# Layer 0 of a convolution-attention hybrid: the first spectral product worked on modes, without a forward transform of q, with a skip matrix from TensorE and image sums in four tiles

## The chip, the cores and the metric

The kernel runs on one core of one Trainium2 chip. The metric is the device time of one execution in microseconds (us). One core has five engines with instruction queues of their own: PE (TensorE, matrix products; PEld are its weight loads), DVE (VectorE), ACT (ScalarE), POOL (GpSimd) and SP (SyncE, which here only issues DMAs). They wait for each other by semaphores.

## What is computed

The input x is [4, 32, 128, 128] in float32: four images of a batch, each with T = 32 channels of 128 x 128 points. Two layers follow each other. Layer 0 is a neural-operator block with attention; layer 1 is an attention and a mixture of experts over tokens. Only layer 0 is concerned here. Cut to what matters, it computes per image of the batch:

```python
def _spectral_conv(x, w):                 # keep 64 x 33 modes, multiply, go back
    X = rfft2(x); Xk = low modes of X
    return irfft2(Xk * w)                 # (for one channel: a product per mode)

x0 = _gn(x)                               # group norm
xn = _inorm(x0)                           # each channel's image to mean 0, variance 1
k, q, v = (_spectral_conv(xn, W) + skip * xn for W, skip in (K, Q, V))   # 32 heads
p_attn = softmax(q . k)                   # between the 32 channels, for each head
p = _spectral_conv(p_attn . v, Pcw) + skip # back from the heads to one
a  = _inorm(p + x0)
an = _inorm(a)
m = gelu(_inorm(_spectral_conv(an, m0cw)) + m0sw * an)
m =      _inorm(_spectral_conv(m,  m1cw)) + m1sw * m
x = x + _inorm(m) + a
```

"The first spectral product" is the one with m0cw. Its input, called q in the kernel (the code reuses the letter for p + x0), is itself a sum: what the attention makes in modes, plus a matrix over the 32 channels times x. So its modes can be had in two ways: by a forward transform of the finished q, or from the attention's own modes plus the same small matrix times the modes of x, which the kernel has from the start of the image.

## The kernel before

All matrix products are float32. A transform is two products with tables in SBUF: over columns, then over rows. The loop `for b in range(B)` (L912) goes through the four images; the front of image b + 1 (its norms and modes) is put into the second half of image b. A tile scheduler sets the order of each engine's queue from the program order and its own costs, and `behind(later, earlier)` adds an order by hand. The parts of one image, in order of time, are these.

- *The mix, u stage* (L955 to L1015). For each of five blocks of 13 (last 12) rows of modes and each of four groups of 8 channels, SP loads the modes of x, broadcast over partitions, as a pair of `xb` (L969, one for the real and one for the imaginary part; the pool holds four pairs), ACT copies them to PSUM as `xw` (L980), POOL (L989) or DVE (L993) multiplies them with the weights `gb` into `u`, and PE sums with the softmax `pr` into `po` (L926). In between PE transposes the image (`pxt`) and multiplies it with the channel matrix `bd` (`sk`), which gives the skip part of q. The pairs are loaded from `xd` in DRAM, written by SP (L559) when the image's modes are ready.
- *py, pv, four* (L1022 to L1048). py goes from channel-major to the layout for the inverse transform (L1027), ACT and DVE copy it to `yf`; `inverse` (L313) makes `pv` (L319) and `four` (L324), and DVE adds the result to q and takes its statistics (L1042, L1044).
- *q's norm and forward transform.* `stats("q", st)` (L258) packs the statistics (`pk`), sums them on PE (`m`) and takes the mean mode apart (`x0`, `flat`, `dq`). `spectra(0, q)` (L1101) transforms q: rows on PE (L305), copies `z`, columns on PE (L1123, `px`), the multiplication by the masks on DVE (L1134, L1137) and the sum on POOL (L1140, `spec`). `weighed` (L1150) gets the variance of the product from the squares (L1085, L1091, L1099) with one more PE sum, `ms`. From it come `r0`, `hq`, `hb`, `hs`, the scales of the gelu.
- *The next image's sums*, `image_rows` (L389): ACT squares (L395), PE sums image and square over blocks (L401, 32 products of 512 columns into two tiles of 32 output rows), ACT copies `ev` (L410), and `image_moments` (L413) spreads them with 16 small products (L419).
- *The gelu stage* (L1195 to L1245). `row_products` (L334, L342) and `four_images` (L353, L358) bring the product back, `gelu(a, g)` adds the skip part on DVE (L1212), ACT applies the gelu (L1216) and DVE takes statistics (L1224). `early` rows of the second transform (L305 with g) go between. `add_attention` (L1076, L1079) adds scaled q to the image, 32 adds in all.
- *The second norm and product.* `stats("gl", st)` again has pk, m and x0; `spectra(1, gl)` transforms g. Beside it the front of the next image runs: `spectra_of_images` (L482) with the column scales `colg` (L448), the products L503, L523, L534, the writes of `xd` (L559) and an edge row (L564), then `attention_weights` (L653): scores, softmax `ph` (L755), `prd` and `pr` through DRAM (L771, L775).
- *The end of the image.* The inverse of the second product (`back`, L360) runs in two halves, a = 0 and a = 1; its results are added to the image (L1334 on POOL, L1399 on DVE) and stored as x1 in four stores of 512 KB (L1422). `skip_matrix` (L780) makes `bd` for the next image from ph: two products cm (L787), two DVE products and two reductions of 512 elements (L791, L792), and bd (L797). It is called after half a = 0.

For image 0 there is no image before it: its front runs alone at the start, and `spread_values` (L629) makes the weights gb for all images from 64 products gw (L638), with copies on DVE and ACT (L644, L646).

Of the kernel before, what the change touches and what calls it, by code (L numbers as in the profile page):

```python
# [36 lines left out]
def _constants():  # L37
# [55 lines left out]
    )  # L93
    return by_p.astype(np.float32), inv_cols.astype(np.float32)
# [5 lines left out]
NCONST = 128 + 128 + NX + 2 * NU + 4 + 32 + 4 + 96 + 64 + P + 32 + 3 * NY + 2 * P  # L100
# [30 lines left out]
def layer0(  # L131
    tc, x, kq_modes, kq_mirror, v_modes, v_mirror, pcw, mcols, mrows, heads, heads_by_row, heads_row, small_row, by_p, inv_cols, dram, x1, first
# [57 lines left out]
    cos_back, sin_back = columns(P), columns(P)  # L190
    par = const.tile([P, NSMALL], F32, name="par")
# [5 lines left out]
    nc.vector.memset(one_of_8[:, 7:8], 1.0)  # L197
    ones = const.tile([P, P], F32, name="ones")
# [59 lines left out]
    def stats(name, st):  # L258
# [11 lines left out]
        m = ps.tile([P, 2, T], F32, name="m", tag="wide")  # L270
# [5 lines left out]

        x0 = ps.tile([P, 2, T], F32, name="x0", tag="wide")
# [23 lines left out]
    def four_rows(images, z, k, copy):  # L301

        pz = ps.tile([P, 4, P], F32, name="pz", tag="a")
        for j in range(4):
            nc.tensor.matmul(pz[:, j], images[k + j], rows, start=True, stop=True)  # L305
        return copy(z[:, k : k + 4], pz)
# [27 lines left out]
    def row_products(spec, a, ahead=(), slots=range(4), wide=None):  # L334

        wide = wide or [ps.tile([P, 2, 512], F32, name="y1", tag="wide") for _ in range(2)]
        for slot in slots:
            c = slice(slot * P, slot * P + P)
            for k, trig in enumerate((cos_back, sin_back)):
                for g in range(4):  # L340
# [8 lines left out]
                    for earlier in ahead:  # L349
                        behind(mm, earlier)  # L350
        return wide
# [37 lines left out]
    def image_rows(xt):  # L389

        products = []
        rows8 = ps.tile([64, 4, C], F32, name="rows8", tag="a")
        for g in GROUPS:
            xx2 = grp.tile([P, GI, C], F32, name="xx2", tag="pr", bufs=6)
            square = nc.scalar.activation(xx2, xt[:, g : g + GI], AF.Square)  # L395
            if "q_r" in roots:
                behind(square, roots["q_r"])
            for h in range(2):
                m = g // 4 + h
                for k, src in enumerate((xt[:, 4 * m : 4 * m + 4], xx2[:, 4 * h : 4 * h + 4])):  # L400
                    mm = nc.tensor.matmul(  # L401
                        rows8[32 * k : 32 * k + 32],
                        one_of_8[:, 7 - m : 39 - m],
                        src,
                        start=m == 0,
                        stop=m == 7,
                    )
                    products.append(mm)
        ev = grp.tile([64, 4, C], F32, name="ev", tag="pr", bufs=6)
        nc.scalar.copy(ev, rows8)  # L410
        return ev, products

    def image_moments(ev):  # L413

        s12 = [ps.tile([P, T], F32, name=f"s{t}", tag="a") for t in "ab"]
        for j in range(4):
            for k in range(2):
                r = slice(32 * k, 32 * k + 8)
                nc.tensor.matmul(s12[k][:, j::4], ev[r, j], ident[r, r], start=True, stop=True)  # L419
# [62 lines left out]
    def spectra_of_images(b, xt, normed, then=None):  # L482
# [6 lines left out]
        xd = dram.tile([T, 2, KX + 1, KY], F32, name=f"xd_{b}")  # L489
        xe = modes.tile([P, KP, T + T // 2], F32, name=f"xe_{b}", tag="xe")  # L490
# [4 lines left out]
        folded = {}  # L495

# [14 lines left out]
        def unfold(a):  # L511
# [44 lines left out]
            nc.vector.tensor_copy(xx[:1, t, 0], bias)  # L556
            for part in range(2):
                for x0 in (32, 0):
                    nc.sync.dma_start(  # L559
                        out=xd[t, part, 32 - x0 : KX - x0].rearrange("t x y -> x t y"),  # L560
                        in_=xx[KX * part + x0 : KX * part + x0 + 32, t, :KY],
                    )

        def edge_row():  # L564
# [6 lines left out]
            nc.vector.tensor_tensor(x32, o32, ysc[:m], ALU.mult)  # L571
            w32 = small.tile([m, T], F32, name="w32", tag="w32")
            nc.vector.tensor_scalar(w32, x32, edge[:m], None, ALU.mult)
            t32 = ps.tile([T, m], F32, name="t32", tag="a")
            nc.tensor.matmul(t32, x32, ident[:m, :m], start=True, stop=True)
            s32 = small.tile([T, 2 * n], F32, name="s32", tag="s32")
            nc.scalar.copy(s32[:, :m], t32)
            nc.sync.dma_start(
                out=xd[:, :, KX], in_=s32.rearrange("t (r y) -> t r y", r=2)[:, :, :KY]
            )  # L580
            return x32, w32
# [22 lines left out]
        return xx, (xe, xm), xd, edges, ysc, by_group  # L604

    def value_weights():
        shape = [P, KX // 4, KA]
        t1, t2 = (prep.tile(shape, F32, name=f"v{n}", tag=f"t{n}") for n in (1, 2))
        for ri, op in enumerate((ALU.add, ALU.subtract)):
            c0 = v_raw[:, :, 0, ri]  # L610
# [301 lines left out]
    for b in range(B):  # L912
# [122 lines left out]
        if b == 0:  # L1035
            mode_tables(weighed_last)
# [1078 lines left out]
```

## Time and profile before

| | us |
|---|---|
| median of 3 runs | 2871.71 (2871.12 to 2872.87) |
| the profiled execution | 2870.23 |
| its span, first to last instruction | 2868.6 |
| layer 0 | 0 to 833 |
| start of py (L1027), images 0 to 3 | 131.55, 323.99, 515.20, 707.76 |
| first gelu (L1216), images 0 to 3 | 186.43, 377.66, 569.29, 764.54 |

The mean clock granted to TensorE is 0.985 of full speed. Where lines of the profile are shown below, a line of the time line reads: start in us from the span's start, busy us, engine, line of the kernel, operation, out <- in, shape of the output <- shape of the input, how many instructions the line sums up, and in brackets how long the engine stood idle ahead of it and what ended that wait. SPq is the issue of DMAs on SP, with the time SP spent issuing, not the transfer's. Durations of products of PE on small tiles overlap, so their mean is longer than the distance between them.

### The profile page before, as it was taken

The numbers are of one execution on the slowest core, as the hardware profiler recorded it, in microseconds if no ns is written. First come the engines' busy times: TensorE is split into PE (matmuls) and PEld (weight loads), VectorE is DVE, ScalarE is ACT, GpSimd is POOL, SyncE is SP. The second block draws the span as 40 slices with busy tenths as digits, with TensorE's granted clock in tenths as the row PEclk, the third lists the DMA queues.
The fourth block names the chain that finished last, engine by engine and source line by source line (L and its number), as shares of the span: only waits on it lengthen the run. The fifth ranks groups of instructions, "written<-read, shape, count | busy, mean of one in ns | idle before, by whom it ended". The sixth has DMA issues, their size and how long they took to land.

```text
span 2868.6 us, 52910 instructions
## 1 busy us (share of the span) xinstructions
PE 2720.7 (95%) x19638; PEld 1379.6 (48%) x19638; DVE 2175.5 (76%) x4830; ACT 2315.7 (81%) x3243; POOL 2035.3 (71%) x1804
## 2 busy tenths in 40 slices
PE   8898999988879999999999999999999999999996
PEld 5565664654644444445444444544444454444442
DVE  5888788778766677777787776778788677877777
ACT  3555466465459999999999999999999999999990
POOL 2706418137028998998998988898898888878872
PEclk9999999999989999999999999999999999999998
DMA  4403204114030101002101000110100010010000
GB/s 103 125 1 106 88 8 149 39 42 138 3 81 23 41 1 41 8 14 47 40 2 34 16 16 19 41 27 23 41 1 16 20 34 19 16 34 1 16 12 19
DMA packets 151153, 107.72 MB, mean 38 GB/s; under 512 B 36302, under 2 KB 140017, under 8 KB 150897
## 3 DMA queue, kind: packets, MB, share of 16 engines
q1 hardware_dynamic: 147633, 102.26, 13.5%
q8 instruction: 155, 2.54, 0.4%
q10 hardware_dynamic: 3264, 2.10, 0.3%
q14 instruction: 101, 0.83, 0.1%
HBM read 63.86 MB, written 19.50 MB: 29 GB/s over the span
## 4 chain that ended last, share of the span: by engine, by line
PE 60%; ACT 7%; DVE 5%; POOL 3%; issue 2%; DMA 0%; SPq 0%; DVEq 0%; POOLq 0%; ACTq 0%
PE d L1869 26%; PE po L1888 15%; PE px L1770 6%; PE n L1869 5%; ACT r L1938 3%; DVE r L1943 1%; ACT e L1954 1%; DVE xc L1779 1%; ACT r L1950 1%; PE pl L1739 1%; POOL e L1946 1%; PE pz L1571 1%; PE pa L1701 1%; PE pt L1533 1%; PE pz L1586 1%
## 5 line engine op out<-in xcount | busy, mean ns | idle before, releaser
L1943 DVE TENSOR_TENSOR r<-n,r 128x1024 f32<-128x1024 f32 (+1 forms) x1056 | 961.9, 953 | 457.3 <-PE n L1869 327.9
L1938 ACT ACTIVATE r<-d 128x1024 f32<-128x1024 f32 (+1 forms) x1056 | 793.6, 803 | 63.6 <-PE n L1869 51.4
L1946 POOL TENSOR_TENSOR e<-r 128x512 f32<-128x512 f32 x528 | 673.4, 1275 | 213.0 <-DVE r L1943 211.4
L1950 ACT ACTIVATE r<-r 128x1536 f32<-128x1536 f32 x528 | 783.6, 1484 | 16.8
L1947 POOL TENSOR_TENSOR e<-e,r 128x512 f32<-128x512 f32 x528 | 671.8, 1272 | 41.4
L1869 PE MATMUL d<-qe,ke 32*128 32x512 f32 (+3 forms) x2304 | 604.5, 601 | 16.9 <-ACT r L1938 12.8
L1869 PE MATMUL n<-qe,ke 32*128 32x512 f32 (+3 forms) x2304 | 604.6, 601 | 0.0
L1888 PE MATMUL po<-e,kx 128*128 128x512 f32 (+3 forms) x1152 | 594.4, 605 | 3.0 <-POOL e L1959 3.0
L1869 PE MATMUL n<-qf,kf 32*128 32x512 f32 (+3 forms) x2304 | 550.8, 553 | 0.0
L1869 PE MATMUL d<-qf,kf 32*128 32x512 f32 (+3 forms) x2304 | 549.1, 552 | 0.0
L1779 DVE SCALAR_TENSOR_TENSOR xc<-px,wgt,xc 128x128 f32<-128x128 f32 x1024 | 354.5, 349 | 34.9 <-PE px L1770 5.2
L1888 PEld LDWEIGHTS po<-e,kx 128*128 128x128 f32 x1152 | 175.4, 188 | 376.1 <-issue 297.6
L1954 ACT ACTIVATE e<-e 128x512 f32<-128x512 f32 x528 | 324.2, 614 | 14.7 <-POOL e L1947 14.7
L1869 PEld LDWEIGHTS d<-qe,ke 32*128 32x128 f32 x2304 | 176.5, 183 | 302.0 <-ACT r L1938 273.2
L1869 PEld LDWEIGHTS d<-qf,kf 32*128 32x128 f32 x2304 | 219.1, 185 | 164.4 <-issue 152.6
L1770 PE MATMUL px<-we,x2t 128*128 128x512 f32 (+3 forms) x644 | 271.0, 515 | 5.7 <-DVE xc L1779 2.0
L989 POOL TENSOR_TENSOR u<-xb,gb 128x858 f32<-128x858 f32 (+1 forms) x112 | 220.6, 2008 | 42.4 <-PE po L926 37.6
L1869 PEld LDWEIGHTS n<-qf,kf 32*128 32x128 f32 x2304 | 227.5, 185 | 24.8 <-issue 17.2
L1140 POOL TENSOR_TENSOR spec<-part,part 128x512 f32<-128x512 f32 x16 | 25.7, 1609 | 284.8 <-DVE gn_r_t L253 93.0
L993 DVE TENSOR_TENSOR u<-xw,gb 128x858 f32<-128x858 f32 (+1 forms) x208 | 215.6, 1105 | 6.7 <-ACT xw L980 3.1
L1770 PEld LDWEIGHTS px<-we,x2t 128*128 128x128 f32 x644 | 119.3, 193 | 140.4 <-issue 116.8
L1869 PEld LDWEIGHTS n<-qe,ke 32*128 32x128 f32 x2304 | 176.8, 183 | 10.9 <-DVE r L1943 1.5
(425 smaller groups left out, 3409.3 us busy)
## 6 DMA issues: line engine op xcount, KB each, us to landing
xb<-xd SPq DMA_DIRECT2D x128, 214.5 KB
xc<-x SPq DMA_DIRECT2D x29, 512.0 KB
x<-x SPq DMA_DIRECT2D x16, 512.0 KB
qf<-qe SPq DMA_DIRECT2D x64, 128.0 KB
out<-xc SPq DMA_DIRECT2D x15, 512.0 KB
x<-in_x SPq DMA_DIRECT2D x14, 512.0 KB
xb<-xd SPq DMA_DIRECT2D x32, 198.0 KB
kf<-ke SPq DMA_DIRECT2D x32, 128.0 KB
```

The source lines that it names most:

```text
L989: weighed = nc.gpsimd.tensor_tensor(u, xb, gk, ALU.mult)
L993: weighed_last = nc.vector.tensor_tensor(u, xw, gk, ALU.mult)
L1770: nc.tensor.matmul(px[:, at_e : at_e + m], x2t[:, k * P : (k + 1) * P], we[:, own[0] : own[0] + m], start=True, stop=True,)
L1779: nc.vector.scalar_tensor_tensor(xc[:, k], px[:, i], wgt[:, k, e : e + 1], xc[:, k], ALU.mult, ALU.add)
L1869: nc.tensor.matmul(o, k, q, start=turn == 0 or g > 0, stop=turn == 1 or g > 0)
L1888: nc.tensor.matmul(sums[c, h][:, q0 : q0 + c1 - c0], kx[:, jb], e[:, c0:c1], start=jb == 0, stop=is_last and q0 > 2 * P, skip_group_check= ...
L1938: nc.scalar.activation(r[:, g], d, AF.Ln, scale=1.0 / DSCALE)
L1943: nc.vector.tensor_tensor(r[:, g], part, r[:, g], ALU.mult)
L1946: nc.gpsimd.tensor_tensor(e, r[:, 1], r[:, 2], ALU.add)
L1947: nc.gpsimd.tensor_tensor(e, e, r[:, 0], ALU.add)
L1950: nc.scalar.activation(r, r, AF.Exp, scale=-1.0)
L1954: nc.scalar.activation(e, e, AF.Exp)
```

## The change

The parts of the diff belong together as follows.

- The front of an image keeps its unscaled modes too: ACT copies them to `plain`, and eight DMAs write them to a second buffer `xu` in DRAM, behind those of `xd`; `edge_row` makes a second edge row for it. In the mix, eight DMAs read them back as `xs`, in the layout of py, put between the loads of xb.
- py accumulates: `rows_of` puts the attention's part into PSUM and has ACT copy it to yf for the inverse, and `first_product` adds `by_part` times `xs` to the same PSUM tile. DVE multiplies it with two columns of the mode table, and POOL adds the two into `modes_of_q`: these are the modes of the first spectral product.
- The forward transform of q, its masks, `dq` and the mean mode of `stats("q")` go. The variance of the product is the sum of the squares of `modes_of_q` (one Square on ACT, one reduction on DVE, two corrections for the zero columns, one PE sum).
- The inverse is made from `modes_of_q` by four channels at a time: pv2 and fours (128 products), in place of `row_products` and `four_images`. The gelus run in the order of channels. The adds of `add_attention` stand at other places: eight ahead of gelu(0), eight after gelu(1), sixteen after the last gelu.
- `image_rows` uses four tiles of 32 output rows, `image_moments` eight products with `one_row`; the squares are made between the copies of yf.
- `skip_matrix` makes cm with 32 products of one column and spreads it by one product with `alike`; it also makes `by_part`, and is called after half a = 1.
- `stats` leaves out the mean mode for q; the tables for masks, mirrors and constants change with these.

Cut to its core:

```diff
-    def image_rows(xt):
+    def image_rows(xt, parts, earlier=None):
...
-                    mm = nc.tensor.matmul(
-                        rows8[32 * k : 32 * k + 32],
+                    r = 64 * k + 32 * (m % 2)
+                    mm = nc.tensor.matmul(
+                        rows8[r : r + 32],
                         one_of_8[:, 7 - m : 39 - m],
                         src,
-                        start=m == 0,
-                        stop=m == 7,
+                        start=m < 2,
+                        stop=m > 5,
...
-                r = slice(32 * k, 32 * k + 8)
-                nc.tensor.matmul(s12[k][:, j::4], ev[r, j], ident[r, r], start=True, stop=True)
+                r = slice(64 * k, 64 * k + 64)
+                nc.tensor.matmul(s12[k][:, j::4], ev[r, j], one_row[r], start=True, stop=True)
...
+            plain = grp.tile([P, half, KY], F32, name="plain", tag="fold")
+            nc.scalar.copy(plain.rearrange("p (k i) y -> p i k y", i=2), std[:, :, :, :KY])
+            unscaled.append((t, plain))
...
+        for t, plain in unscaled:
+            to_rows(xu, t, plain)
+        store_edge(*edge_rows[1])
...
-            cm = ps.tile([P, T, 16], F32, name="cm", tag="a")
-            mm = nc.tensor.matmul(cm, pv[r].to_broadcast([NH, P]), ph[r], start=True, stop=True)
...
+            for t in range(16):
+                j = 32 * (t % 4)
+                mm = nc.tensor.matmul(
+                    cm[j : j + 32, t // 4 : t // 4 + 1], ph[r, :, t], pv[r], start=True, stop=True
+                )
...
+        nc.tensor.matmul(cp[:, 0], alike, by_four.rearrange("p h k j -> p (h k j)"), start=True, stop=True)
+        nc.vector.scalar_tensor_tensor(cp[:, 1], cp[:, 0], own, same, ALU.mult, ALU.add)
...
+                if x0 and by_images:
+                    to, of = by_images.pop(0)
+                    nc.sync.dma_start(out=to, in_=of)
...
+            copied = nc.scalar.copy(yf[:, :, :, y0 : y0 + n].rearrange("p t r y -> p y r t"), pys[y0])
...
+        def first_product(y0):
...
+                    nc.tensor.matmul(
+                        py[r, k], xs[r, :, y0 + k], by_part[r], start=False, stop=k == n - 1, skip_group_check=True
+                    )
...
+            nc.vector.tensor_tensor(one_, py, table[:, :, :1].unsqueeze(3).to_broadcast(shape), ALU.mult)
+            nc.vector.tensor_tensor(
+                two, py[:, :, ::-1], table[:, :, 1:].unsqueeze(3).to_broadcast(shape), ALU.mult
+            )
+            nc.gpsimd.tensor_tensor(
+                modes_of_q[:, :, :, y0 : y0 + n].rearrange("p t r y -> p y r t"), one_, two, ALU.add
+            )
...
+        nc.scalar.activation(squares, modes_of_q.rearrange("p t r y -> p t (r y)"), AF.Square)
...
+        nc.vector.tensor_reduce(by_t, squares, AX.X, ALU.add)
...
+        energy_of = sums("ms", ones, by_t, "b")
...
-        spec, sq = spectra(0, q)
-        ahead = []
-        if b + 1 < B:
-            ev, ahead = image_rows(loaded)
-        v0 = weighed("v0", sq, squares, layers[0][2], "a")
-        if ahead:
-            behind(summing["ms"], ahead[-3])
...
+        for k in range(4):
+            inverse_of(k)
+        add_attention(0)
+        gelu(0)
+        if b + 1 < B:
+            ev, _ = image_rows(loaded, next_squares, roots["gelu"])
+            sv = image_moments(ev)
+        gelu(1)
+        add_attention(GI, roots["gelu"])
+        inverse_of(4)
+        inverse_of(5)
+        gelu(2)
+        gelu(3)
+        inverse_of(6)
+        inverted = inverse_of(7)
+        for k in range(4, 8):
+            gelu(k)
+            early_rows(k - 4)
...
-        for g in GROUPS:
-            add_attention(g)
+        for g in GROUPS[2:]:
+            add_attention(g, roots["gelu"])
...
-            if a == 0 and b + 1 < B:
-                bd = skip_matrix(weights[2], front[4], inverted)
+            if a and b + 1 < B:
+                bd, by_part = skip_matrix(weights[2], front[4], rows_last)
```

## Prediction, made before the changed kernel ran

> **What bounds the kernel now.** I read the busy totals first, then busy time by stretches of one image, then the time lines of single engines. TensorE is busy 95% of the span, but only layer 0 (0 to 833 us) is touched; layer 1 is an unchanged program that starts later or earlier as a block. So the question is how long one image of layer 0 takes. Image 1, from the start of its py products at 131.55 to the same products of image 2 at 323.99, takes 192.4 us. Cut at the points where the chain changes hands (columns: stretch, length, busy PE, PE load, DVE, ACT, POOL with counts, clock, DMA share, GB/s):
>
> ```profile
> PE 2720.7 (95%) x19638; PEld 1379.6 (48%) x19638; DVE 2175.5 (76%) x4830; ACT 2315.7 (81%) x3243; POOL 2035.3 (71%) x1804
> ```
>
> ```profile
> 131.55:158.70 27.15, 25.82 (x284) 24.58 (x285) 18.36 (x73) 7.10 (x10) 0.00 (x0) 1.00 0.01 2
> 158.70:186.40 27.70, 26.14 (x273) 15.57 (x271) 23.54 (x94) 13.11 (x25) 3.45 (x2) 1.00 0.00 1
> 186.40:203.60 17.20, 13.89 (x120) 8.67 (x122) 15.24 (x66) 15.43 (x40) 0.00 (x0) 1.00 0.01 1
> 203.60:234.00 30.40, 28.58 (x321) 23.49 (x312) 24.89 (x101) 14.73 (x48) 4.36 (x4) 0.97 0.07 11
> 234.00:265.50 31.50, 26.69 (x286) 13.16 (x284) 22.86 (x33) 20.95 (x49) 23.44 (x14) 0.98 0.46 109
> 265.50:324.00 58.50, 52.63 (x643) 25.74 (x642) 54.08 (x53) 36.17 (x82) 51.02 (x26) 1.00 0.56 172
> ```
>
> The reader is to see that the first two and the fourth stretch are carried by TensorE (over 94% busy), the third by DVE and ACT (the gelus), and the last by DVE and POOL together: a pause there isn't caught up. In the time line these lines are the joints:
>
> ```profile
> 131.55 8.03 PE L1027 MATMUL py<-cst,rs 128*64 128x64 f32 x132 [0.61 <-ACT rs L1013]
> ...
> 158.71 0.20 DVE L263 TENSOR_TENSOR pk<-st 128x32 f32<-128x32 f32 x1
> ...
> 179.96 0.38 PE L383 MATMUL ms<-v_s,ones 128*128 128x32 f32 x2
> ...
> 186.43 3.19 ACT L1216 ACTIVATE g<-g,hb,hs 128x128 f32<-128x128 f32 x8
> ...
> 204.99 0.40 PE L271 MATMUL m<-pk,ones 128*128 128x64 f32 x2
> ```
>
> q is normed at 158.71, but the first gelu waits until 186.43, because the variance of the spectral product (ms, 179.96) comes only after q's forward transform (L305, L1123) and next to the next image's sums (L401, 32 records). From the start of py to the first gelu the four images take 54.9, 53.7, 54.1 and 56.8 us.
>
> At the other end of the image, on SP's queue and on DVE:
>
> ```profile
> 238.29 7.79 SPq L969 DMA_DIRECT2D xb<-xd  x8
> 254.84 2.96 SPq L771 DMA_DIRECT2D prd<-ph  x4
> 258.54 1.64 SPq L775 DMA_DIRECT2D pr<-prd  x2
> 260.28 1.08 SPq L1422 DMA_DIRECT2D x<-x  x2
> 263.24 1.22 SPq L969 DMA_DIRECT2D xb<-xd  x2
> 267.07 2.20 SPq L1422 DMA_DIRECT2D x<-x  x2
> ```
>
> ```profile
> 257.28 0.69 DVE L791 TENSOR_TENSOR cd<-cm,sel 128x512 f32<-128x512 f32 x1 [0.43 <-PE cm L787]
> ...
> 260.94 1.97 DVE L797 TENSOR_TENSOR bd<-cst,cp 128x128 f32<-128x128 f32 x1
> ...
> 266.96 8.71 DVE L993 TENSOR_TENSOR u<-xw,gb 128x858 f32<-128x858 f32 x9
> ```
>
> Four pairs of xb are loaded ahead of the softmax, and the skip matrix (257.28 to 262.9) stands in front of the last four adds, so the unbroken run of u products starts at 266.96.
>
> **What the Trainium skill says.** "TensorE: Matmul & The Clock Gate", Architectural detail: DVE and ACT take their queues strictly in order. So an add that isn't urgent delays everything behind it; the trace agrees (the adds at 262.84 come straight after bd). The same page, Part 3, Measured speedup: three column tiles give 2.38 times. In the trace the two 32-column tiles of L401 already run in pairs, 0.43 us apart. "DMA: Bandwidth & Descriptors", Issuing engines are not separate DMA queues: all transfers share the 16 DMA engines and interleave. The trace agrees so far as two 512 KB stores and the xb loads around them share the stretch of DMA share 0.46 to 0.56.
>
> **The change part by part**, against the profiled run (2870.23 us, span 2868.6).
>
> 1. *py to q's norm: +5.* 66 more products of two records each go into the same PSUM as py. 132 records of py took 8.03 us; 64x64 records elsewhere go at 0.026 (32 of em in 0.83), so these cost 132 x 0.026 = 3.4 to 8.0; I take 5. They stand ahead of the pv products on PE, so q is late by this. The two DVE multiplications of each group (0.68 each) and the POOL add (1.27 to 2.18) run beside PE's next products. q's norm: T + 27.2 + 5 = T + 32, with T the start of py.
>
> 2. *From the norm to the first gelu: -14.* The transform of q goes: 32 row products (7.1 us of PE), px (4.3), the two row products' place ahead of the gelus, the masks, weights and reduction on DVE. The variance is now a Square of 2112 elements on ACT and a reduction on DVE (about 2.1 and 2.3 us, scaled from 1.05 for 1024 and 1.21 for 1024), and ends during q's own inverse. What is left is the chain of small operations: m, three inverse roots (each about 2.5 us, as 161.94 to 164.5), pk and m (1.6), some ten DVE steps of 0.2, what eight adds between them push aside (about 1.4), the table load 1.28: pk + 13.8 against pk + 27.7. So the first gelu comes at T + 45.8: 9.1, 7.9 and 8.3 us earlier for images 0 to 2. The next image's sums in four column tiles (32 records, about 4 instead of 8.4 us of PE) and half as many moment products stand beside this.
>
> 3. *The gelu stage: +0.8.* 17.16 us become about 18: eight adds (0.265) and the inverse of pv2 and fours (128 records, 14.2 us of PE against 11.1) come in; DVE and ACT had 1.8 us free each, PE 3.3. Last gelu: 8.3, 7.1 and 7.5 us earlier, 22.9 in sum.
>
> 4. *Adds ahead of the second norm: +3.3 for each of three images.* The order of DVE now has 14 adds of groups 2 and 3 behind the last statistics and before pk: 14 x 0.265 = 3.7 us. PE's m, at 204.99 now, waits, and behind it in PE's order the rest of the transform of g and the next image's front, in a stretch where PE is 94% busy. Bounds 1 (PE still has row products when g ends) and 4. Sum 9.9.
>
> 5. *End of the attention: +2.3 for each of three images.* Behind the eight xd writes eight more writes (xu, the unscaled modes) and an edge row are put; they run 8 us more (1.0 us each, as xd), before the softmax is done, at no cost. But the scheduler now has only one pair of xb ahead of the four x1 stores; the others stand behind them. The skip matrix, now 32 one-column products and small DVE steps, stands behind the last adds, so the stores can go at about 261 instead of 267. 2 MB at the 280 GB/s that the trace reaches take 7.5 us, a pair of xb (429 KB) 1.5, and 1.5 from issue to landing: the second pair is there at 270.5, copied at 271.5. DVE has done three u by then, of 52: 49 x 1.1 from 271.5 ends at 325.4 to 326.3, against 324.0. Bounds 0 and 7. Sum 6.9. For image 0 there are no stores.
>
> 6. *Reads of xs in the u stage: +0.3 an image, 1.2.* Eight reads of 135 KB go between the xb; DMA share there is 0.56. Bounds 0 and 6 in sum.
>
> 7. *Start, image 0: +4.* Now gw (L638) starts at 52.08 before the softmax is done, and po follows:
>
> ```profile
> 52.08 3.00 PE L638 MATMUL gw<-g,picked 128*128 128x264 f32 x12
> ...
> 68.19 1.13 PE L787 MATMUL cm<-ph,pv 32*128 32x512 f32 x4
> ...
> 74.08 3.79 PE L926 MATMUL po<-u,pr 128*32 128x429 f32 x16 [2.39 <-DVE u L993]
> ```
>
> In the changed order cm and cp stand before gw on PE, so gw waits for the softmax: start 59 to 61.5, 7 to 9 late. Off that come the skip matrix's 4 us behind gw (69.93 to 73.1) and about 1 of the sums in four tiles. Bounds 2 and 7.
>
> 8. *Last image: -5.4.* First gelu 9 earlier; 16 adds before pk cost up to 4.2, of which I take 3.6, since m was at 789.14 for other reasons: layer 1's first products stand ahead of it on PE.
>
> Sum: -22.9 + 9.9 + 6.9 + 1.2 + 4 - 5.4 = -6.3, so 2863.9 for the profiled run. The median of the runs shown is 1.5 above it: **2865**.
>
> **Rivals.** (A) *The losses are hidden.* PE's own work falls by about 8 us an image (7.1 + 4.3 for q's transform, 1.0 for its small products, 4.4 for sums and moments, less 5 for the first product, 3.1 for the inverse and 1.0 for the skip matrix), and if PE fills what DVE and SP leave, parts 4 and 5 fall to 1 and 0: 16.8 - 3 = 13.8 less, 2851. For it: three of six stretches are over 94% PE. Against: m and the u stage wait by order. (B) *The lost prefetch decides, slower.* One mechanism: the four stores of 2 MB ahead of the second pair of xb, at SP L1422's place. If the last adds end at 267 as now, because PE's inverse and not the skip matrix paces them, the second pair lands at 267.07 + 7.5 + 1.5 + 1.5 = 277.6 less up to 3.7 for the half stored before, and the u products stand for 9 us an image in place of 2.3: 3 x 6.7 = 20 more, 2885. It decides from 2.3 + 6.3 / 3 = 4.4 us an image. For it: the adds before 257 show waits for PE four of 0.15 to 0.79, and 264.80 one of 0.68. Against: those waits are short. (C) *The first product paces q.* POOL's add writes with a stride that no row shows; if it takes 4 us instead of 1.6, five groups take 20 us, the modes and with them the variance end after q's norm, and part 2 loses 5 us an image: 2885. (D) The change moves work, and gains and losses cancel to within 5 us: about 2871.
>
> **How the numbers follow.** A measurement tells about 0.2% (5.7 us) from no change. The forecast has 0.40 (its own range 2856 to 2876 from the bounds of parts 1, 4 and 7), A 0.20, B 0.20, C 0.08, D 0.12. Faster: A whole, 0.24 of the forecast, 0.02 of the others: 0.46. Within 0.2%: 0.13 of the forecast and 0.07 of D: 0.20. Slower: B, C and the rest: 0.34. The range goes from 2846, some way below A's time, to 2886 just above B and C.
>
> **What would show it.** Step 1 and 2: the first gelu 45 to 47 us after py's start, against 54. Step 4: pk about 3.7 us behind the last gelu's statistics, with PE waiting at m. Step 5: DVE and POOL idle after the first u products, released by xb or its copy. Step 7: gw at 60. I would be wrong if the py stretch grew by more than 9 us, or if the u stage of images 1 to 3 grew by over 4.

## The result, and the profile after

The changed kernel takes 2919.48 us (median of 4 runs, 2918.2 to 2920.41) against 2871.41 (2870.45 to 2872.87) for the kernel before: a ratio of 1.0167, 95% interval 1.0149 to 1.0184. It is 48 us slower; the forecast of 2865, its range and its sign were wrong. The profiled span is 2918.6 us. From its page:

```profile
PE 2723.5 (93%) x19686; PEld 1413.3 (48%) x19686; DVE 2150.4 (74%) x4800; ACT 2320.6 (80%) x3225; POOL 2049.8 (70%) x1816
...
DMA packets 170338, 114.34 MB, mean 39 GB/s; under 512 B 54462, under 2 KB 158177, under 8 KB 170081
```

No engine has much more to do than before: PE +3 us, DVE -25, ACT +5, POOL +14. So the 50 us of span are waits, or the same work at a lower clock. (The DMA packets of under 512 bytes rose from 36302 to 54462, the bytes by 6%.) Image 1 once more by stretches, cut at the same events as in the table below (columns: stretch, length, busy PE, PE load, DVE, ACT, POOL with counts, clock, DMA share, GB/s):

```profile
142.40:181.20 38.80, 36.55 (x430) 34.52 (x431) 23.25 (x73) 15.20 (x19) 5.45 (x5) 1.00 0.01 1
181.20:190.30 9.10, 8.31 (x64) 4.47 (x63) 7.54 (x42) 3.58 (x9) 0.00 (x0) 1.00 0.01 2
190.30:213.70 23.40, 19.41 (x150) 18.09 (x150) 18.61 (x80) 16.57 (x41) 0.00 (x0) 0.78 0.00 1
...
241.90:278.90 37.00, 32.08 (x391) 16.73 (x391) 22.44 (x44) 23.44 (x54) 22.83 (x14) 0.95 0.76 75
278.90:346.00 67.10, 53.27 (x640) 26.24 (x640) 54.05 (x53) 37.93 (x84) 54.04 (x27) 0.92 0.64 189
```

py starts at 142.4, 346.0, 552.7 and 757.9 (before: 131.6, 324.0, 515.2, 707.8). Layer 1 is as long as before, to about 1.5 us. What the prediction expected of each part, and what the two time lines show:

| part of layer 0 | predicted, us | measured, us |
|---|---|---|
| start, to py of image 0 | +4 | +10.9 |
| py to first gelu, images 0 to 2 | -25.3 | -7.0 -5.4 -6.0 = -18.4 |
| first to last gelu, images 0 to 2 | +2.4 | +6.2 +6.2 +6.2 = +18.6 |
| last gelu to first po of the next image | +9.9 | +3.2 +6.3 +5.3 = +14.8 |
| first po to py (u stage), images 1 to 3 | +7.8 | +8.7 +8.3 +7.2 = +24.2 |
| image 3, py to the last store | -5.4 | +1.3 |
| sum | -6.6 | +51.4 |

(The reads of xs for image 0 are in the first row's measurement, with 0.3 of the prediction left out of the second column. The rows are read from one profiled execution of each kernel.) Two rows make the result. The gelu stage gives away what the stretch before it had won. And the u stage of image 1, where DVE is busy 54.05 us as it was before (54.08), is 67.1 us long instead of 58.5, which is 8.6 us more of idle DVE; in images 2 and 3 the stage grows by 8.3 and 7.2 us.

*The gelu stage.* PE's time line and ACT's, after:

```profile
188.92 0.59 PE L429 MATMUL rows<-xx,one_of 128*32 128x512 f32 x1
192.48 0.38 PE L449 MATMUL sa<-one_row,ev 64*128 64x8 f32 x1 [2.98 <-ACT ev L438]
...
194.64 3.25 PE L1337 MATMUL pv<-cst,modes 128*66 128x128 f32 x14 [0.28 <-DVE sv L452]
197.68 1.48 PE L1350 MATMUL fours<-icol,v 66*128 66x128 f32 x8
```

```profile
190.31 1.65 ACT L1361 ACTIVATE g<-g,hb,hs 128x128 f32<-128x128 f32 x4 [0.63 <-DVE g L1357]
191.87 0.56 ACT L438 COPY ev<-rows 128x512 f32<-128x512 f32 x1
192.33 1.65 ACT L1361 ACTIVATE g<-g,hb,hs 128x128 f32<-128x128 f32 x4
196.65 0.58 ACT L1345 COPY v<-pv 66x512 f32<-66x512 f32 x1 [2.67 <-PE pv L1337]
...
199.90 3.19 ACT L1361 ACTIVATE g<-g,hb,hs 128x128 f32<-128x128 f32 x8
```

The image sums are done at about 189.5, but their copy `ev` is ordered behind gelu(0). PE's next instructions in order are the small products that need ev (8 products; a float32 product shows as two records, so 16 records), and PE stands for 2.98 us, and the inverse of the next channels stands behind those. Then PE runs slowly:

```profile
191.00:194.00 3.00, 1.52 (x15) 1.52 (x16) 2.89 (x13) 2.98 (x8) 0.00 (x0) 0.62 0.00 0
194.00:198.00 4.00, 3.72 (x20) 3.63 (x21) 3.61 (x17) 0.58 (x1) 0.00 (x0) 0.50 0.00 0
```

At half the clock pv takes 3.25 us for 14 records, and ACT has no gelu between 194.0 and 199.9.

*The u stage of image 1.* SP's queue, DVE, POOL and ACT, after:

```profile
271.92 1.29 SPq L1061 DMA_DIRECT2D xb<-xd  x2
...
274.24 4.42 SPq L1572 DMA_DIRECT2D x<-x  x4
278.70 6.84 SPq L1061 DMA_DIRECT2D xb<-xd  x8
285.65 0.40 SPq L1072 DMA_DIRECT2D xy<-xu  x1
```

```profile
279.77 1.04 DVE L1088 TENSOR_TENSOR u<-xw,gb 128x858 f32<-128x858 f32 x1
287.16 2.01 DVE L1088 TENSOR_TENSOR u<-xw,gb 128x858 f32<-128x858 f32 x2 [6.35 <-ACT xw L1075]
289.90 4.54 DVE L1088 TENSOR_TENSOR u<-xw,gb 128x858 f32<-128x858 f32 x4 [0.73 <-ACT xw L1075]
```

```profile
286.66 14.97 POOL L1084 TENSOR_TENSOR u<-xb,gb 128x858 f32<-128x858 f32 x7 [7.82 <-DMA xb<-xd]
```

```profile
285.27 0.52 ACT L1075 COPY xw<-xb 128x429 f32<-128x429 f32 x1 [7.95 <-DMA xb<-xd]
```

Only one pair of xb stands ahead of the four stores of x1. The second is issued at 278.70, and the copy that waits for it starts at 285.27. The releaser of DVE, ACT, is itself released by a load, so the load is what counts. This is rival B's place; but the first wait is only 6.35 of the 8.6 us (5.87 and 5.62 in images 2 and 3), and the experiments show that it moves when it is removed.

The stores don't come earlier either. These are DVE's last adds, before and then after:

```profile
266.36 0.68 DVE L1399 TENSOR_TENSOR x<-x,four 128x512 f32<-128x512 f32 x1
```

```profile
272.85 1.48 DVE L1546 TENSOR_TENSOR x<-x,four 128x512 f32<-128x512 f32 x2 [3.04 <-PE four L378]
...
275.68 0.69 DVE L1546 TENSOR_TENSOR x<-x,four 128x512 f32<-128x512 f32 x1 [0.17 <-PE four L378]
```

They end 63.4 us behind the last gelu before and 62.7 after, although the skip matrix now stands behind them: they wait for PE.

*The start.* PE, after:

```profile
60.34 0.64 PE L856 MATMUL cp<-by_four,cst 128*128 128x32 f32 x2 [0.29 <-DVE by_four L849]
62.14 2.13 PE L691 MATMUL gw<-g,picked 128*128 128x264 f32 x4 [1.16 <-DVE g L678]
66.09 17.54 PE L691 MATMUL gw<-g,picked 128*128 128x264 f32 x60 [1.83 <-DVE g L678]
83.56 0.91 PE L1009 MATMUL po<-u,pr 128*32 128x429 f32 x4
```

gw starts at 62.1 (before: 52.08) and ends at 83.6 (68.3); po follows. Ahead of these lines PE stands 5.25 us for the softmax, which cm needs.

### The profile page after: what moved, and what is told of

It is laid out like the page before. It is cut to its first block, busy times and chain, and to the rows that moved or that the text cites. A ratio compares the mean times of both kernels' runs of the same rounds, so it can differ in the third digit from the quotient of the medians.

```text
span 2918.6 us, 53043 instructions
## 1 busy us (share of the span) xinstructions
PE 2723.5 (93%) x19686; PEld 1413.3 (48%) x19686; DVE 2150.4 (74%) x4800; ACT 2320.6 (80%) x3225; POOL 2049.8 (70%) x1816
## 2 busy tenths in 40 slices
DMA packets 170338, 114.34 MB, mean 39 GB/s; under 512 B 54462, under 2 KB 158177, under 8 KB 170081
## 4 chain that ended last, share of the span: by engine, by line
PE 70%; ACT 9%; DVE 9%; POOL 6%; issue 3%; DMA 1%; SPq 1%; DVEq 0%; POOLq 0%; ACTq 0%
PE d L2019 26%; PE po L2038 15%; PE px L1920 6%; PE n L2019 5%; ACT r L2088 3%; POOL u L1084 3%; PE po L1009 2%; DVE r L2093 1%; ACT e L2104 1%; PE py L1128 1%; DVE xc L1929 1%; PE py L1147 1%; PE pz L309 1%; DMA xb<-xd 1%; ACT r L2100 1%
## 5 line engine op out<-in xcount | busy, mean ns | idle before, releaser
L1920 PE MATMUL px<-we,x2t 128*128 128x512 f32 (+3 forms) x644 | 270.5, 513 | 6.2 <-DVE xc L1929 2.6
L2019 PEld LDWEIGHTS n<-qf,kf 32*128 32x128 f32 x2304 | 227.5, 185 | 23.6 <-issue 16.6
L1009 PE MATMUL po<-u,pr 128*32 128x429 f32 (+1 forms) x1280 | 150.8, 549 | 52.5 <-POOL u L1084 50.9
```

The lines of the kernel that those rows point to most:

```text
L1920: nc.tensor.matmul(px[:, at_e : at_e + m], x2t[:, k * P : (k + 1) * P], we[:, own[0] : own[0] + m], start=True, stop=True,)
L2019: nc.tensor.matmul(o, k, q, start=turn == 0 or g > 0, stop=turn == 1 or g > 0)
```

## The experiments

Each takes the changed kernel, or where it says so the kernel before, and differs by the diff shown. Ratios are against the kernel before in the same batch, with their 95% intervals.

**The start: weights before the skip matrix.**

```diff
+        return mm
...
-    spread_values(picked, weights[5], weights[4], weights[7])
-    bd, by_part = skip_matrix(weights[2], front[4])
+    spread = spread_values(picked, weights[5], weights[4], weights[7])
+    bd, by_part = skip_matrix(weights[2], front[4], spread)
```

> Image 0 only: the skip matrix's products stand behind the 64 gw products on PE, as before the change. Theory (order of gw): gw starts at 52 to 53 instead of 62.1, the first po comes near 75 instead of 83.6, and the time falls by 7 to 11 us, to 2908 to 2912. Rival (the softmax's way through DRAM is late by itself, pr was issued 8.3 us after prd here against 3.7 elsewhere, behind the xu writes): gw starts early but po still waits for pr or xb, and the time falls by less than 4 us.

2916.56 us (2912.35 to 2919.51), ratio 1.0154 [1.0138, 1.0169].

```profile
55.39 2.10 PE L691 MATMUL gw<-g,picked 128*128 128x264 f32 x4 [4.08 <-DVE g L678]
...
76.17 0.98 PE L845 MATMUL cm<-pv,ph 32*32 32x1 f32 x64
```

gw starts 6.7 us earlier, and py of image 0 at 136.0 instead of 142.4: 6.4 of the 10.9 us at the start are this order. In the median 3 us are left of them, which is inside the spread of the runs, so the 7 to 11 of the theory don't show in the time.

**The gelu stage: ev no longer behind gelu(0).**

```diff
-            ev, _ = image_rows(loaded, next_squares, roots["gelu"])
+            ev, _ = image_rows(loaded, next_squares)
```

> The order that holds the copy of the image sums (ev) behind the first four gelus is left out. Theory (ev chain): the moments, and behind them on PE the inverse of channels 16 to 23, start 2 to 3 us earlier, PE doesn't fall idle from 189.5 to 192.5, its clock doesn't drop to 0.5, and the gelu stage shrinks from 23.4 to 18 to 20 us in images 0 to 2: 10 to 16 us less, 2904 to 2910. Rival (the clock is low in this stretch whatever PE does, and DVE's adds and gelu sums bound the stage): less than 5 us.

2918.27 us (2913.19 to 2921.37), ratio 1.0159 [1.0144, 1.0174]. The stage shortens about as the theory had it, from 23.4, 23.4 and 22.5 to 18.5, 20.7 and 18.5 us, yet the time falls by 1 us. By stretches, this kernel, gelu stage of image 0 and u stage of image 1:

```profile
190.70:209.20 18.50, 16.24 (x130) 14.21 (x131) 17.04 (x76) 16.16 (x41) 0.00 (x0) 0.91 0.01 1
...
276.90:343.90 67.00, 54.35 (x641) 26.12 (x641) 54.40 (x53) 38.70 (x84) 54.41 (x27) 0.90 0.64 188
```

The order of ev is shown to be the main cause of the longer stage. But part of the gain is lost at once: the first gelu comes 1.2, 2.3 and 1.0 us later after py, so that from py to the last gelu only 3.7, 0.4 and 3.0 us are won. Little of that reaches the end: py of image 1 starts 2.1 us earlier (0.7 of it from the start), and the u stage is as long as it was.

**The adds: behind the next image's scales.** The sixteen adds of groups 2 and 3 after the last gelu are ordered behind `normed[4]`, the last scale made for the next image's front.

> The sixteen adds of groups 2 and 3 stand behind the scales of the next image's front instead of ahead of the second norm. Theory of the prediction (adds ahead of pk cost 3.3 us an image): the column scales colg and the front of the next image come 3 to 4 us earlier, 9 to 12 us less. Rival (the front waits for the row products of g on PE anyway, colg came only 0.3 us later than before the change): within 4 us of no change.

2916.17 us (2916.03 to 2917.66), ratio 1.0155 [1.0138, 1.0172]. That is 3 us in the whole program, at most 1 us an image and not 3.3; it lies within the 4 us of the rival. In image 0 m comes 3.7 us sooner behind the last gelu (2.4 instead of 6.1), but the column scales colg only 1.2 us sooner.

**The u stage: the prefetch given back.** The eight writes of xu and the edge row of images 1 to 3 move from the front of the image to behind the loads of the u stage's first block.

```diff
-        for t, plain in unscaled:
-            to_rows(xu, t, plain)
-        store_edge(*edge_rows[1])
+        def write_unscaled():
...
+            if b and x0 == 0:
+                front[7]()
```

> The writes of the unscaled modes (xu) of images 1 to 3 are put behind the xb of the first block, so that four pairs of xb are loaded before the softmax again; nothing else changes. Theory (the lost prefetch): the u stage of images 1 to 3, 66.5 to 67.1 us from the first to the last po now against 57.8 before, falls back to 57 to 59 us, and the time falls by 22 to 28 us, to 2891 to 2898. Rival (the xs reads and the doubled writes load the DMA engines, and the u stage is slow through them): the stage stays above 63 us and the time falls by less than 10 us.

2909.12 us (2909.02 to 2910.2), ratio 1.013 [1.0115, 1.0145]: 10 us of the 22 to 28 expected. The u stages don't shorten: 67.0, 66.4 and 66.0 us. So these 10 us lie in other stretches, and which part of the edit gave them wasn't found. SP and DVE in this kernel:

```profile
277.86 3.00 SPq L598 DMA_DIRECT2D xu<-plain  x2
280.90 0.64 SPq L628 DMA_DIRECT2D xu<-s  x1
281.65 1.90 SPq L1067 DMA_DIRECT2D xb<-xd  x3
285.49 0.32 SPq L1078 DMA_DIRECT2D xy<-xu  x1
```

```profile
278.06 6.79 DVE L1094 TENSOR_TENSOR u<-xw,gb 128x858 f32<-128x858 f32 x7
289.30 2.97 DVE L1094 TENSOR_TENSOR u<-xw,gb 128x858 f32<-128x858 f32 x3 [4.45 <-ACT xw L1081]
293.63 2.01 DVE L1094 TENSOR_TENSOR u<-xw,gb 128x858 f32<-128x858 f32 x2 [1.35 <-ACT xw L1081]
```

The first wait is gone, and another comes at 289.30: now the fifth pair of xb stands behind the stores and the writes of xu, issued at 281.65. More waits for xw follow, of 1.35, 3.11 and 1.41 us. So the depth of the prefetch alone doesn't decide; the place in the whole line of transfers of this stage is the next suspect. The next kernels move the others in that line: the reads of xs (`xy` in the trace) and the stores.

**All reads of xs behind the last block's loads.**

```diff
-                if x0 and by_images:
+                for _ in range(2 if x0 == 4 * NK else 0):
                     to, of = by_images.pop(0)
-                    nc.sync.dma_start(out=to, in_=of)
+                    behind(nc.sync.dma_start(out=to, in_=of), broadcast)
```

> The eight reads of xs per image are pinned behind the xb of the last block, where DVE and POOL no longer wait for loads; all else as in the changed kernel. With the prefetch back, the u stage had stayed at 66 us and DVE had waited for xw, and xw for xb, until 316 us. Theory (the reads of xs, each ahead of an xb on SP's queue and on the DMA engines, starve the copies): the u stage of images 1 to 3 falls from 66.5 to 60 to 63 us and the time by 10 to 20 us. Rival (the backlog behind the four stores does it alone): the stage falls by less than 2 us.

2930.64 us (2929.71 to 2935.72), ratio 1.0209 [1.0194, 1.0225]: 11 us worse, where neither theory nor rival had a loss. DVE still waits 6.33 us near the start of image 1's stage, and its last block now waits too (1.99 us at 349.4); the stages take 70.2, 71.4 and 67.7 us. Image 0, which has no stores, also has its py 4 us later (146.5).

**The same with the prefetch given back** (both edits above).

> Both: four pairs of xb ahead of the softmax, and the reads of xs in the last block. Theory (each of the two only moves the wait to the other's place, the loss needs both undone): the u stage comes back to 57 to 60 us, 22 to 28 us less than the changed kernel. Rival (the doubled writes xu, which now stand between the stores and the next xb, take over): the stage stays above 62 us, with DVE waiting for xw near 285 us.

2913.69 us (2908.64 to 2914.83), ratio 1.0143 [1.0127, 1.016]: 17 us better than the kernel with late reads, where the same prefetch had been worth 10 with the reads in between. But the u stages take 65.4, 65.1 and 64.4 us, not 57 to 60: the theory falls, and the rival's number holds. In image 1 DVE waits 4.71 us for xw until 294.7, and the pair concerned was issued at 286.95, behind the stores and the writes of xu. Stores and writes share that place, so this run alone doesn't say which of them counts.

**The stores of x1 one by one behind the loads of the second block, reads late, prefetch as in the changed kernel.**

```diff
+                if x0 == NK and stores:
+                    b_, i_, x_ = stores.pop(0)
+                    behind(
+                        nc.sync.dma_start(out=x1[b_, i_].rearrange("t w c -> w t c"), in_=x_[:, i_]), broadcast
+                    )
...
-                stored = nc.sync.dma_start(out=x1[b, i].rearrange("t w c -> w t c"), in_=xr[:, i])
                 if b + 1 < B:
-                    behind(stored, weights[3])
+                    stores.append((b, i, xr))
```

> The reads of xs in the last block, and the four x1 stores of images 0 to 2 put one by one behind the xb of the second block, so that no xb stands behind 2 MB of stores; xb are still not loaded ahead of the softmax. Theory (the stores' place is what the lost prefetch costs): the u stage comes to 58 to 61 us, 18 to 25 us less than the changed kernel. Rival (the stage is slow by xs alone): no better than with the reads late alone.

2917.51 us (2913.23 to 2921.43), ratio 1.016 [1.0145, 1.0175]: 13 us better than with late reads alone, so the rival falls. The u stages take 64.2, 61.7 and 67.0 us; the 58 to 61 of the theory are not reached. The first wait is gone here without the prefetch: the place of the stores had made it.

**All of it together:** prefetch, late reads, stores between, and the edits of the start, of ev and of the adds.

> All edits together: prefetch, reads of xs late, stores behind the second block's xb, gw ahead of the skip matrix, ev free of the gelus, adds of groups 2 and 3 behind the front's scales. If the parts add up (25 for the u stage, 4 to 8 for gw, 5 to 10 for the gelu stage, 3 for the adds): 2872 to 2882, level with the kernel before. If the gains of the first part of the image then show in full: below 2865.

2886.49 us (2886.27 to 2894.1), ratio 1.0059 [1.0044, 1.0074]: 33 us better than the changed kernel, but 4 us above the 2872 to 2882 of the sum. The u stages take 62.7, 64.6 and 63.7 us in the profiled execution, the slowest of the four; in image 1 DVE waits 3.15 us for xw in the last block, where the reads are.

**The same, with the reads of xs in the third and fourth block instead of the last.**

> All edits together again, but the reads of xs lie one by one behind the xb of the third and fourth block: in the last block they had delayed the last pairs by about 2.6 us in every image. Theory (the loss of the u stage is the waiting line of loads on SP and the DMA engines, wherever the extra 1 MB of reads and the stores stand close to an xb that is short): the u stage of images 1 to 3 comes to 57.5 to 60 us from 62, the time to 2868 to 2878. Rival (the extra 1.6 MB of transfers an image costs its time wherever it stands): 62 us stay, 2882 to 2890.

2877.38 us (2872.18 to 2884.35), ratio 1.002 [1.0013, 1.0026]: 42 of the 48 us are back. SP's queue and DVE at the place of the waits shown above:

```profile
268.11 1.21 SPq L1069 DMA_DIRECT2D xb<-xd  x2
269.43 0.40 SPq L1084 DMA_DIRECT2D x<-x  x1
272.37 1.21 SPq L1069 DMA_DIRECT2D xb<-xd  x2
```

```profile
271.17 24.39 DVE L1101 TENSOR_TENSOR u<-xw,gb 128x858 f32<-128x858 f32 x23
298.46 2.01 DVE L1101 TENSOR_TENSOR u<-xw,gb 128x858 f32<-128x858 f32 x2 [2.90 <-ACT xw L1088]
```

23 products run without a wait, with a store between the pairs of xb of the second block. The u stages take 61.1, 59.8 and 59.5 us, against 67.1, 66.7 and 66.7 in the changed kernel and 58.4, 58.5 and 59.5 before: 20 of the 24 us that this stage had lost are back. The edits of the start, of ev and of the adds had given 3, 1 and 3 us each by itself, so by that sum most of the 42 is the place of the transfers; the three transfer edits without the other three weren't run. This kernel moves the same bytes in the same number of packets as the changed one (114.34 MB, 170338): what cost the u stage its time was mostly the order of the transfers, not their number. The place of the reads alone is worth about 9 us (2886.49 to 2877.38, the two in different batches).

**What the gelu stage is worth once the loads don't wait:** the last kernel with ev behind gelu(0) again.

> e8_mid with one of its edits undone: the copy ev of the image sums stands behind the first gelu again, as in the changed kernel. e3_ev_early took this order away from the changed kernel and the gelu stage fell from 23 to 19 us, yet the time by 1 only. Theory (the gelu stage costs, and in e3_ev_early its gain was taken back by the loads of the u stage, which are freed here): each of the images 0 to 2 is 3.5 to 5 us longer than in e8_mid, gelu stage 22 to 23.5 us, time 2888 to 2893. Rival (the stage has slack behind it anyway, since the second norm and the next image's scales wait for something else): time within 3 us of e8_mid's 2877.

2881.85 us (2881.65 to 2884.87), ratio 1.0042 [1.0028, 1.0056], 4 us more than without, 1.5 us an image. The profiled executions can't be set against each other to the microsecond, since that of the kernel without this order is the slowest of its 20 runs (2884.35). Gelu stage and u stage of this kernel:

```profile
184.10:206.70 22.60, 18.66 (x150) 17.07 (x150) 18.46 (x78) 16.61 (x41) 0.00 (x0) 0.85 0.00 1
...
269.90:329.60 59.70, 53.71 (x642) 26.04 (x640) 53.27 (x54) 37.83 (x82) 51.64 (x26) 1.00 0.69 206
```

The stages are 22.6, 22.9 and 22.8 us again, instead of 18.5, 20.9 and 20.4, but the first gelu comes 1.1, 2.6 and 1.2 us earlier after py; image 0 to image 1 takes 193.5 us instead of 192.4. So a good part of the longer stage is made up ahead of it: from py to the last gelu the three images differ by 3.0, -0.6 and 1.2 us, about the 4 us of the time in sum. What is absorbed behind the stage these two profiles don't show. The rival (within 3 us) comes nearer than the theory (2888 to 2893); neither range was met.

**The same again with the image sums in two tiles** (ev early).

> e8_mid with the image sums in two tiles again (32 records in pairs, 8.4 us of TensorE instead of 5.7, 16 small products over 8 rows instead of 64). Theory (the shorter sums leave TensorE idle ahead of the first gelu, and its granted clock falls for the next 10 us, as b2_rows4 showed on the kernel before): the clock of the gelu stage rises to over 0.9, first gelu at most 1 us later after py, image cycles 0.5 to 2 us shorter, time 2870 to 2876. Rival (the sums stand in the way of the inverse here, since q's transform no longer gives them cover): first gelu 2 to 3 us later in each image, time 2883 to 2890.

2880.98 us (2877.57 to 2882.24), ratio 1.0032 [1.0021, 1.0044]. The clock of the gelu stage is 0.92 where it was 0.91, and the time isn't lower. The theory falls: no harm from four tiles shows in this kernel. The rival falls too, as the first gelu comes 1.1, 2.6 and 1.2 us earlier after py, not later.

**Parts of the change by themselves, on the kernel before.** First the new skip matrix (cm by 32 products of one column, spread by one product), at its old place and without by_part:

> The kernel before with the new skip matrix alone (32 one-column products, small DVE steps, one spreading product), at its old place behind half a = 0; no by_part. Theory: the stretch on DVE from 257.3 to 262.9 shrinks by 3 to 4 us for images 1 to 3, the last adds, the stores and the u products start that much earlier, and the time falls by 8 to 12 us below the kernel before. Rival (32 products and a second round trip to PE take the same 5 us, or the u products wait for po and loads anyway): within 3 us of the kernel before.

2866.52 us (2864.06 to 2868.94), ratio 0.9979 [0.997, 0.9988]: 5 us faster than the kernel before in the same batch (2871.81), less than the 8 to 12 of the theory.

```profile
258.26 0.77 DVE L809 TENSOR_TENSOR bd<-cst,cps 128x128 f32<-128x128 f32 x1
261.66 1.48 DVE L1411 TENSOR_TENSOR x<-x,four 128x512 f32<-128x512 f32 x2 [2.62 <-PE four L360]
```

bd is done at about 259 instead of 262.9, and then DVE waits 2.62 us for PE: the adds are paced by PE's inverse. bd ends 3.9 us earlier, but the first u product after it only 1.2 (264.23 instead of 265.40, of which 0.6 come from an earlier start), and an image takes 0.6 to 1.5 us less.

Then the image sums in four tiles, alone:

> The kernel before with the image sums in four tiles and half the moments alone. PE's sums shrink from 8.4 to about 3.5 us an image. If PE's work in that stretch sets the first gelu (it is 94% busy): the first gelu of images 0 to 2 comes 3 to 4 us earlier, 9 to 13 us less. If the chain of the product's variance on DVE sets it (its last reduction ended at 179.0, and ms was at 179.96): less than 3 us.

2875.6 us (2872.35 to 2879.48), ratio 1.0012 [1.0004, 1.002]: 4 us slower, by an interval just clear of 1. This kernel, PE's time line at the sum that follows, and stretches of it:

```profile
179.08 0.38 PE L388 MATMUL ms<-v_s,ones 128*128 128x32 f32 x2 [2.12 <-DVE v_s L1170]
```

```profile
175.00:180.00 5.00, 2.88 (x56) 1.78 (x52) 4.96 (x13) 0.89 (x2) 1.87 (x1) 1.00 0.00 0
180.00:186.00 6.00, 6.00 (x49) 3.90 (x44) 5.70 (x32) 2.88 (x7) 0.00 (x0) 0.52 0.01 3
```

The sums go from 8.4 to 5.4 us of PE, and nothing was waiting for them: PE now waits for DVE, and then runs at a clock of 0.52 where the kernel before had 1.00. The first gelu comes 1.4, 0.8 and 2.4 us later after py than before in images 0 to 2.

Last, both together:

> Both of these on the kernel before: the sum of the two if they are independent, as they lie in different stretches of the image.

2871.9 us (2869.15 to 2874.94), ratio 1.0 [0.9992, 1.0009]: the two cancel. The new product on modes by itself, with the old sums and the old skip matrix, was not run.

## Why the prediction was wrong

The steps that failed are 5 and 6, the end of the attention and the reads of xs, sized at 2.3 and 0.3 us an image and measured at 7.2 to 8.7 together. That loads come late behind other transfers was right; three terms of the sum were not.

- Step 5 let the stores go some 6 us earlier, since the skip matrix leaves their way. The last adds, which the stores need, end only 0.8 us earlier behind the last gelu, because PE's inverse paces them. Rival B had said so, and the new skip matrix alone shows it by itself. With that, the first wait is 6.35, 5.87 and 5.62 us. (Step 5's own terms, 261 + 7.5 + 1.5 + 1.5, also add up to 271.5 for the second pair, not 270.5.)
- Behind that wait I let DVE run unbroken. Another 2 us or so of the loss are later waits, and new ones came when the first was removed.
- Step 6 put the reads of xs at 0.3 us an image, with the mean DMA share of 0.56 beside it. Their place alone moved the time by about 9 us in the whole program.

Rival B has the right size for the u stage, 9 us, but its one mechanism, the lost prefetch, doesn't carry it: with the prefetch back the u stages stay at 66 to 67 us. It took a new place for stores, writes and reads together to bring them back to within 3 us of the kernel before (2.7, 1.3 and 0.0 us more).

In the table step 3 is off by about as much, 16 us over three images, as steps 5 and 6 are. I put it second because taking its cause away gave back 1 and 4 us only. Both signs that the prediction named for being wrong came true: the stretch from py to q's norm grew by more than 9 us, and the u stage by over 4.

Point by point:

- Step 1, py to q's norm, +5, measured +9.6 in image 0 (to m). py takes 16.8 us for 264 records where it took 8.03 for 132. In the time line of after (columns as above):

```profile
142.41 3.99 PE L1128 MATMUL py<-cst,rs 128*64 128x64 f32 x64 [0.61 <-ACT rs L1108]
146.33 2.08 PE L1147 MATMUL py<-by_part,xy 64*64 64x64 f32 x32
```

A record of the new product costs 0.065 us, as much as one of py with twice the depth, not the 0.026 of em. The 8.8 us more for py are above even the upper bound of 8.0.
- Step 2, norm to first gelu, -14, measured -16.6 (end of m to gelu(0): 25.7 to 9.1 us). This step was right and a little better than forecast, so its mechanism holds, with one slip: the small products of the sums aren't halved, as both kernels have 8 of them (16 records), now over 64 rows instead of 8; steps 1 and 2 together made -7.0, -5.4 and -6.0 in place of -9.1, -7.9 and -8.3.
- Step 3, the gelu stage, +0.8, measured +6.2. I counted the inverse's records at full clock and didn't see that the copy of the sums is ordered behind gelu(0) and holds PE's queue, which then runs at half the clock. With that order taken away the stage is 18.5, 20.7 and 18.5 us, near the forecast 18 in two images. Little of it reaches the end, as removing it from two kernels gave 1 and about 4 us.
- Step 4, the adds, +3.3 an image. m comes 4.7 us later behind the last gelu, and PE waits 1.61 us for it, as the step has it; but moving the adds gave 3 us in all, so the front of the next image must wait for other work too. The row of +14.8 is larger than step 4. Of it 6.9 lie ahead of the first write of xd and 7.9 behind; in the latter DVE waits 0.8, 1.3 and 3.4 us for a copy of xb ahead of its first u, so part of it belongs to the loads again. The rest I can't divide.
- Step 7, the start, +4, measured +10.9: gw is 10 later, as the step's 7 to 9 had it nearly, but what should come off didn't. Its 64 records end 15 later, since they stop for 1.83 us after the first four and run at a low clock (0.50 from 56 to 72 us, where the kernel before has 1.00 up to 68 and 0.93 after). 6.4 of it is the order, shown by the kernel with gw first.
- Step 8, the last image, -5.4, measured +1.3: its first gelu is 5.6 earlier instead of 9, its gelu stage 3.2 longer, and 3.6 more are lost from the last gelu to the store.
- Rival A (all losses hidden) and D are refuted by the time. C, a slow strided add on POOL, is refuted by its row: 1.27 to 1.29 us each.

What remains open is why the rearranged kernel with 42 us back isn't faster than the kernel before. In the median it is 6 us slower. Its profiled execution is its slowest, with a span 13.9 us longer: 6.4 of these are in the start and 2.4 in the last image. Its first gelu is 3 to 6 us earlier in each image, and that lead is gone by the first write of xd in two images of three: the gelu stage is 1.3, 3.7 and 4.0 us longer than before, and the stretch from there to xd about 2 us. No run here singled out the reason.

## What to carry to other kernels

When a change adds transfers to a stage, write down the whole queue of that stage in order, loads, stores and writes, and ask for each load that is needed soon what stands ahead of it; the first stall isn't the sum. Ask too what paces the stores ahead of it. A copy ordered behind a stage's first instruction is a wait of the engine whose queue holds its reader, and everything behind that reader. And work taken off an engine is worth something only where the next thing is ready: try the parts alone, since of the two tried here one was a gain and one a small loss, and the whole was far worse than both.

## What the runs showed of the hardware

Several traces show a granted clock of half of full speed for some us, soon after PE had waited, in a program in which PE is over 90% busy. In stretches of 2 us the clock falls to 0.50 after waits of 2.98 us (changed kernel, 192 to 198 us) and 3.04 (ev late again, 188 to 192), of 2.12 (four tiles alone, 182 to 186) and of 1.67 (ev early, 196 to 198). In the gelu stage of the kernel before, the waits are at most 1.17 us and the clock stays at 1.00, though PE is idle for 19% of it.

The length of a single wait doesn't decide it. With sums in two tiles again, 0.50 (200 to 202) followed a wait of 1.02. And with four tiles alone PE has, near 200 us, the same waits as in the kernel before (0.71, 0.89 and 0.78 us against 0.71, 0.90 and 0.78), and yet its clock is 0.50 from 202 to 204 where the kernel before has 1.00. That waiting is the cause wasn't tried by itself, and what decides between the two remains open.

A record of a product on 64 x 64 tiles that adds to an existing sum took as long here as one of 128 x 64 (0.065 and 0.062 us), while the 64 x 64 records of em go at 0.026 (32 in 0.83 us). Which of the differences between the two counts wasn't tried.
